# The last image's normalisation: eight rows a group, six groups loaded ahead, buffers of the scan's states, sums on VectorE

## Chip, cores and metric

The kernel runs on one core of a Trainium2 chip. TensorE (PE) multiplies matrices, VectorE (DVE), ScalarE (ACT) and GpSimd (POOL) work elementwise, and SyncE (SP) issues nearly all DMAs here; 16 DMA engines move the data between DRAM and the on-chip memory (SBUF). The metric is the device time of one execution in microseconds (us), lower is better. All data is 32-bit float.

## What is computed

The input `x` has 8 images of 128 channels with 128 x 128 points. Layer 0 (a dilated convolution, an attention over channels in the Fourier domain and a gate) gives a new `x`, which the kernel keeps in DRAM as `x1`, one tensor for each image. Layer 1 is a 3 x 3 convolution, a small state-space scan over 8 tokens of 16 channels at each point, and a group normalisation with SiLU and a residual. The change is at the end of layer 1:

```python
def _L1_conv_ref(x, ...):
    y = conv(x, conv_w) + conv_b
    seq = y.reshape(B * H * W, TOKEN_NUM, GCN)      # 8 tokens of 16 channels
    out = _mamba(seq, ...)                          # the scan
    xr = out.reshape(B, C, H, W)
    g = xr.reshape(B, GROUPS, C // GROUPS, H, W)    # 4 groups
    mu = g.mean((2, 3, 4), keepdims=True)
    var = g.var((2, 3, 4), keepdims=True)
    g = (g - mu) / jnp.sqrt(var + EPS)
    xp = g.reshape(B, C, H, W) * gn_w[None, :, None, None] + gn_b[None, :, None, None]
    xp = jax.nn.silu(xp)
    return x + xp
```

Mean and variance go over a whole image, so no row of an image can be normalised before its last row is out of the scan.

## The kernel before

Channels lie on the 128 partitions. Layer 1 works through 256 blocks of RB = 4 rows (512 elements a partition), 32 blocks an image, in a software pipeline: for each block number i, `step(i, s)` is called for s = 2 to 11 and then `seam(i)`. One call works on several blocks at once; block i is in its scan while i + 3 is in its convolution and i - 1 in its projection out. The loop stands in a manual schedule of all five engines: each engine's instructions keep the order in which the program calls them, and so do SP's DMAs. The loop over i runs from -4 to nb + 1 = 257 (nb = 256). The last block is 255; it leaves the scan in step 256.

The names that matter:

- `project_out` (L881 and on) brings a finished block into `xr` (ScalarE copy, L891). `keep` takes its statistics (VectorE, L898) and stores it to the DRAM tensor `gn` of its image (L899); it is called in the seam of the next block.
- `norm_of(b)` (L902 to L925) is called in step s = 2, two blocks after the last of an image. It makes a scale `sc` and an offset `bi` of the statistics, in small instructions on VectorE, TensorE and ScalarE, and appends the image's 32 blocks to the list `tails`.
- `last_load` takes one block off `tails`: it loads `v` from `gn` (L931) and `res` from `x1` (L932). `last_act` makes SiLU(v * sc + bi) in place on ScalarE (L937). `last_sum` adds it to `res` on GpSimd (L941) and stores `res` to the output (L942). `v` and `res` come from the pool `wk2`, with two buffers of 4 rows each.

During the scan one tail block is done for each scan block: `last_load` at s = 8, `last_act` in the seam, `last_sum` at s = 9 of the next block. So the 32 blocks of image 6 go along with blocks 225 to 256. Image 7, the last, has no scan to go along with: one of its blocks starts in step 257, and the loop `while tails or fin` (L1095), which stands outside the manual schedule and is ordered by the framework's scheduler, does the others. In the built program it comes out in rounds of two blocks: a store, a load of `v`, a store, a load of `v`, then two loads of `res`.

The scan's states `h` and the weighted states `hc` have pools of their own, `hp` and `hcp` (L682, L683), each with seven buffers of 128 partitions x 1024 elements (4 KB a partition). Nothing uses them after the last block's scan.

In both built programs each DMA that SP issues carries one of eight completion semaphores in turn, and where that isn't implied by another wait it waits for the DMA that had the same one before.

Of the kernel before, what the change touches and what calls it, by code (L numbers as in the profile page):

```python
# [9 lines left out]
F32 = mybir.dt.float32  # L10
AF = mybir.ActivationFunctionType
# [5 lines left out]
P = 128  # L17
C = 128
H = 128
W = 128  # L20
# [121 lines left out]
def layer0(ctx, tc, x, w0, c0, x1):  # L142
# [67 lines left out]
    def first_load(p):  # L210
        for b, xt in enumerate(first_rows()):
            nc.vector.memset(xt[:, 0:3, :], 0.0)
            nc.sync.dma_start(xt[:, 3:RX, :], x[2 * p + b, :, 0:RX - 3, :])
# [366 lines left out]
    gram = p_g.tile([P, P], F32, name="gram")  # L580
    E = mybir.EngineType
    with tc.manual_schedule(engines={E.PE, E.Activation, E.DVE, E.Pool, E.SP}):
        first_load(0)
# [6 lines left out]
def layer1(ctx, tc, x1, w1, c1, out):  # L590
# [12 lines left out]
    nc = tc.nc  # L603
# [9 lines left out]
    def cf(name):  # L613
        at, n = C1[name]
        return ct[:, at:at + n]

    def wf(name):
        at, n = W1[name]
        return wt[:, at:at + n]
# [19 lines left out]
    with tc.tile_pool(name="l1_prep", bufs=2) as prep:  # L639
# [18 lines left out]
        for hf in range(NH):  # L658
            for l in range(L):
                k = hf * L + l  # L660
# [14 lines left out]
    RB = 4  # L675
# [6 lines left out]
    hp = ctx.enter_context(tc.tile_pool(name="l1_h", bufs=7))  # L682
    hcp = ctx.enter_context(tc.tile_pool(name="l1_hc", bufs=7))  # L683
# [6 lines left out]
    nb = len(blocks)  # L690
    st8 = [{} for _ in blocks]
    xins, stats, gns, tails = {}, {}, {}, []
# [6 lines left out]
    def misc():  # L699
        return p_m.tile([P, RB, W], F32, name="pm")  # L700
# [67 lines left out]
    def lay_du(i, hf):  # L768


        d = st8[i]
        du = wk2.tile([P, LP, N], F32, name="du")
        for q in range(NG):
            for k, v, g in ((0, d["dt", hf], q), (8, d["u", hf], (q + GP) % NG)):
                nc.sync.dma_start(du[q * DI + k:q * DI + k + 8], v[g * DI:(g + 1) * DI, :])
        d["du", hf] = du
# [125 lines left out]
    def norm_of(b):  # L902

        mv = wk2.tile([P, 2], F32, name="mv")
        gmv = wk2.tile([P, 2], F32, name="gmv")
        dv = wk2.tile([P, 1], F32, name="dv")
        sc = wk2.tile([P, 1], F32, name="sc")
        bi = wk2.tile([P, 1], F32, name="bi")
        nc.vector.bn_aggr(mv, stats[b])
        ps = misc().rearrange("p a b -> p (a b)")  # L910
        nc.tensor.matmul(ps[:, 0:2], cf("group"), mv, start=True, stop=True)
        nc.vector.tensor_copy(gmv, ps[:, 0:2])
        nc.vector.tensor_sub(dv, mv[:, 0:1], gmv[:, 0:1])
        nc.vector.tensor_mul(dv, dv, dv)
        ps = misc().rearrange("p a b -> p (a b)")
        nc.tensor.matmul(ps[:, 0:1], cf("group"), dv, start=True, stop=True)
        nc.vector.tensor_scalar(sc, ps[:, 0:1], gmv[:, 1:2], GN_EPS, ALU.add, ALU.add)
        nc.scalar.activation(sc, sc, AF.Sqrt)
        nc.vector.reciprocal(sc, sc)
        nc.vector.tensor_mul(sc, sc, wf("gn_w"))  # L920
        nc.vector.tensor_mul(bi, gmv[:, 0:1], sc)
        nc.vector.tensor_sub(bi, wf("gn_b"), bi)
        tails.extend((b, r, sc, bi) for r in range(0, H, RB))

    fin = {}  # L925

    def last_load():
        b, r, sc, bi = tails.pop(0)
        v = wk2.tile([P, RB, W], F32, name="v")
        res = wk2.tile([P, RB, W], F32, name="res")  # L930
        nc.sync.dma_start(v, gns[b][:, r:r + RB, :])  # L931
        nc.sync.dma_start(res, x1[b][:, r:r + RB, :])  # L932
        fin["loaded"] = b, r, sc, bi, v, res

    def last_act():
        b, r, sc, bi, v, res = fin["active"] = fin.pop("loaded")
        nc.scalar.activation(v, v, AF.Silu, bias=bi, scale=sc)  # L937

    def last_sum():
        b, r, sc, bi, v, res = fin.pop("active")  # L940
        nc.gpsimd.tensor_add(res, res, v)  # L941
        nc.sync.dma_start(out[b, :, r:r + RB, :], res)  # L942
# [86 lines left out]
    def seam(i):  # L1029


        now, nxt = live(i), live(i + 1)

        def taps(k0, k1):
            if live(i + 3):
                conv(i + 3, k0, k1)

        spreads([(i, 13)], [(i + 1, 1)])
        exps(i, 13)
        if now:  # L1040
            ends_sum(i, 1)
            decay(i, 12)
            add(i, 12)
            weigh(i, 11, 5)
            weigh(i, 12, 7)
        if nxt:
            lay_states(i + 1, 1, 0)
        taps(5, 6)
        if "loaded" in fin:
            last_act()  # L1050
        if live(i + 2):
            project_x(i + 2)
        if now:
            decay(i, 13)
            add(i, 13)
            weigh(i, 13, 7)
        inject(i + 1, 1)
        if live(i + 2):
            project_z(i + 2)
        spreads([(i, 14)], [(i + 1, 2)])  # L1060
        exps(i, 14)
        if now:
            ends_inputs(i, 1)
        if live(i - 1):
            keep(i - 1)
        inject(i + 1, 2)
        taps(6, 8)
        spreads([(i, 15)], [(i + 1, 3)])
        exps(i, 15)
        if now:  # L1070
            collect(i, 4)
            last_decay(i, 14)
            weigh(i, 12, 6)
        inject(i + 1, 3)
        taps(8, 9)
        if now:
            last_decay(i, 15)
        spreads([(i + 1, 2)], [(i + 1, 4)])
        exps(i + 1, 2)
        inject(i + 1, 4)  # L1080
        if now:
            collect(i, 5)
            weigh(i, 13, 6)
        if live(i + 3):
            turn(i + 3)
        if nxt:
            lay_du(i + 1, 1)

    E = mybir.EngineType
    with tc.manual_schedule(engines={E.PE, E.Activation, E.DVE, E.Pool, E.SP}):  # L1090
        for i in range(-4, nb + 2):
            for s in range(2, 12):
                step(i, s)
            seam(i)
    while tails or fin:  # L1095
        if "active" in fin:
            last_sum()
        elif "loaded" in fin:
            last_act()
        else:  # L1100
            last_load()


def network(tc, x, w0, w1, c0, c1, out):
    B = x.shape[0]
    with tc.tile_pool(name="dram", bufs=1, space=DRAM) as dram:
        x1 = [dram.tile([C, H, W], F32, name=f"x1_{b}") for b in range(B)]
        layer0(tc, x, w0, c0, x1)
        layer1(tc, x1, w1, c1, out)
# [73 lines left out]
```

## Time and profile before

| | us |
|---|---|
| median of three runs | 14719.64 (14719.61 to 14726.95) |
| the profiled execution | 14712.15 |
| its span, first to last instruction | 14710.4 |
| last block's `xr` copied out (ScalarE, L891) | 14577.85 to 14578.44 |
| `sc` and `bi` ready (VectorE, L922) | 14584.02 |
| first load of image 7's `v` issued (SP, L931) | 14578.84 |
| end of the span | 14710.4 |

The profile is one execution. All times in it are counted from the span's start. A stretch table gives for each stretch of time how long each engine was busy; the chain of waits follows the work that ended last backwards, from each instruction to what released it. Lines such as L941 are lines of the kernel before.

Around the turn from scan to tail, SP's own list of issues reads (start, length of the issue, engine, line, operation, destination and source, count):

```profile
14574.26 0.34 SPq L942 DMA_DIRECT2D out<-res  x1
14578.47 0.32 SPq L899 DMA_DIRECT2D gn<-xr  x1
14578.84 0.42 SPq L931 DMA_DIRECT2D v<-gn  x1
14579.35 0.40 SPq L932 DMA_DIRECT2D res<-x  x1
14581.93 0.34 SPq L942 DMA_DIRECT2D out<-res  x1
14582.36 0.38 SPq L931 DMA_DIRECT2D v<-gn  x1
```

The first store is of the last block but one of image 6, the second line is block 255 going to `gn`, then come the loads of the first block of image 7, the store of image 6's last block, and the next load.

### The profile page before, as it was taken

How to read it: one execution, taken by the hardware profiler on the slowest of the kernel's cores; microseconds unless marked ns; L12 is line 12 of the kernel's file. 1: busy time of each engine (PE TensorE's matmuls, PEld its weight loads, DVE VectorE, ACT ScalarE, POOL GpSimd, SP SyncE). 2: the span in 40 equal slices, each digit the busy share in tenths (PEclk: the TensorE clock that was granted, in tenths of full speed). 3: DMA queues.
4: the chain of work that ended last, by engine and by line, in shares of the span. 5: the costliest groups of instructions: out<-in, count | busy, mean ns of one | idle time of the engine just before them, and what ended most of it. 6: DMA issues, size and time to landing. Idle time of an engine off the chain costs nothing. (4 is left out here: it accounts for less than half of the span.)

```text
span 14710.4 us, 200914 instructions
## 1 busy us (share of the span) xinstructions
PE 14255.2 (97%) x70696; PEld 5593.5 (38%) x70696; DVE 12679.2 (86%) x12417; ACT 8295.0 (56%) x9234; POOL 12984.8 (88%) x7076
## 2 busy tenths in 40 slices
PE   9999999999999999999999999999999999999996
PEld 6676653333333333333333333333333333333331
DVE  3343359999999999999999999999999999999995
ACT  3354355555656565555556565656556565656553
POOL 6666669999999999999999999999999999999996
PEclk9999999999999999999999999999999999999996
DMA  4444456666666666666666666666666666666665
GB/s 136 140 136 125 129 123 121 120 122 121 134 135 137 139 134 138 135 139 133 139 135 138 135 138 137 135 140 134 138 136 138 135 138 136 135 137 136 138 135 140
DMA packets 1091886, 1976.02 MB, mean 134 GB/s; under 512 B 125760, under 2 KB 256832, under 8 KB 1082688
## 3 DMA queue, kind: packets, MB, share of 16 engines
q1 hardware_dynamic: 1090304, 1960.82, 61.7%
q8 instruction: 563, 9.22, 0.2%
q14 instruction: 443, 3.63, 0.1%
q10 hardware_dynamic: 576, 2.35, 0.0%
HBM read 419.16 MB, written 201.33 MB: 42 GB/s over the span
## 5 line engine op out<-in xcount | busy, mean ns | idle before, releaser
L846 POOL TENSOR_TENSOR hc<-h,cc 128x1024 f32<-128x1024 f32 x3584 | 8375.5, 2368 | 257.5 <-DVE h L840 223.9
L806 ACT ACTIVATE da<-da 128x1024 f32<-128x1024 f32 x3584 | 3618.7, 1010 | 4024.4 <-PE ups L801 2347.3
L816 DVE TENSOR_TENSOR h<-ups,bb 128x1024 f32<-128x1024 f32 x3584 | 4362.1, 1217 | 239.6 <-PE ups L801 164.6
L801 PE MATMUL ups<-du,m_u 16*128 16x512 f32 x14336 | 4118.2, 642 | 3.1 <-DMA du<-u 1.2
L801 PE MATMUL da<-du,m_a 16*128 16x512 f32 x14336 | 4064.6, 643 | 3.7 <-DVE h L840 2.6
L840 DVE TENSOR_TENSOR h<-da,h 128x1024 f32<-128x1024 f32 x2304 | 2820.5, 1224 | 79.1
L832 DVE TENSOR_TENSOR da<-da,h 128x1024 f32<-128x1024 f32 x2304 | 2819.4, 1224 | 4.6 <-ACT da L806 1.1
L134 PE MATMUL pm<-xin,l_wt 128*128 128x508 f32 (+1 forms) x4608 | 2411.0, 623 | 176.8 <-ACT xr L891 170.1
L838 POOL TENSOR_TENSOR h<-ah,h 128x1024 f32<-128x1024 f32 x768 | 1818.6, 2368 | 442.3 <-DVE ah L830 402.2
L801 PEld LDWEIGHTS da<-du,m_a 16*128 16x128 f32 x14336 | 1078.1, 184 | 2467.3 <-issue 1018.1
L867 PE MATMUL yps<-hc,l_ct 128*32 128x512 f32 x14336 | 1929.1, 610 | 1.0 <-POOL hc L846 1.0
L134 PEld LDWEIGHTS pm<-xin,l_wt 128*128 128x128 f32 x4608 | 751.0, 189 | 1618.3 <-issue 1393.5
L801 PEld LDWEIGHTS ups<-du,m_u 16*128 16x128 f32 x14336 | 1130.0, 183 | 372.6 <-DVE h L816 319.4
L806 ACT ACT_TABLE_LOAD x774 | 993.0, 1283 | 30.2 <-PE ups L801 1.3
L830 DVE TENSOR_TENSOR ah<-da,h 128x1024 f32<-128x1024 f32 x768 | 931.6, 1213 | 0.0
L851 DVE TENSOR_TENSOR hc<-da,hc 128x1024 f32<-128x1024 f32 x512 | 623.8, 1218 | 281.2 <-ACT da L806 280.3
L759 POOL TENSOR_TENSOR u<-dt,xc 128x512 f32<-128x512 f32 x512 | 653.4, 1276 | 186.5 <-ACT dt L754 186.5
L867 PEld LDWEIGHTS yps<-hc,l_ct 128*32 128x32 f32 x14336 | 283.7, 108 | 1375.9 <-issue 816.1
L754 ACT ACT_TABLE_LOAD x511 | 655.6, 1283 | 33.1 <-PE pm L752 5.1
L823 POOL TENSOR_TENSOR cb<-bb,cc 128x512 f32<-128x512 f32 x512 | 656.6, 1282 | 11.7 <-DMA cc<-bc 11.7
L886 PEld LDWEIGHTS pm<-m_o,ym 128*128 128x128 f32 x4096 | 517.6, 191 | 317.2 <-issue 316.5
L752 PE MATMUL pm<-xc,m_dt 128*128 128x512 f32 x1024 | 584.7, 653 | 1.5 <-issue 0.8
(180 smaller groups left out, 14528.9 us busy)
## 6 DMA issues: line engine op xcount, KB each, us to landing
bb<-bc SPq DMA_DIRECT2D x2048, 256.0 KB
cc<-bc SPq DMA_DIRECT2D x2048, 256.0 KB
du<-dt SPq DMA_DIRECT2D x2048, 64.0 KB
du<-u SPq DMA_DIRECT2D x2048, 64.0 KB
xin<-x SPq DMA_DIRECT2D x152, 768.0 KB
xin<-x SPq DMA_DIRECT2D x112, 640.0 KB
gn<-xr SPq DMA_DIRECT2D x256, 256.0 KB
v<-gn SPq DMA_DIRECT2D x256, 256.0 KB
```

Of the source, the lines that this page charges most:

```text
L134: nc.tensor.matmul(out[:, a:b, wa:wb], wt[:, t, :], src[:, r + dy + a - base:r + dy + b - base, wa + dx:wb + dx], start=(n == 0), stop=(n ...
L754: nc.scalar.activation(d["dt", hf], ps, AF.Softplus, bias=wf("dt_b"))
L801: nc.tensor.matmul(o, w, v, start=True, stop=True)
L806: nc.scalar.activation(da, da, AF.Exp)
L816: nc.vector.tensor_mul(h, d["ups", s], state_row(i, "bb", s // GP))
L823: nc.gpsimd.tensor_mul(d["cb", hf], d["bb", hf][:, lp, :], d["cc", hf][:, lp, :])
L830: nc.vector.tensor_mul(d["ah"], da, before)
L832: nc.vector.tensor_mul(da, da, before)
L838: nc.gpsimd.tensor_add(h, d["ah"], h)
L840: nc.vector.tensor_add(h, d["da", s], h)
L846: nc.gpsimd.tensor_mul(hc, d["h", s], state_row(i, "cc", t))
L867: nc.tensor.matmul(d["yps"][g * DI:(g + 1) * DI], gather[:, t % LP, :], d["hc", GP * t + g // GP][:, g % GP], start=False, stop=(t in (3, ...
```

## The change

The loop over i ends at nb = 256, so step 257 is gone. What is left of image 6 (its last block, loaded and activated in step and seam 256) is summed and stored first, in a short loop on `fin`. Image 7 is then done in 16 groups of TR = 8 rows (1024 elements a partition, 512 KB each): `tail_load` loads a group into one buffer of `hp` (under the name `h`) and one of `hcp` (`hc`); `tail` makes the SiLU on ScalarE, the sum on VectorE in place of GpSimd, and the store. Six groups are loaded before `norm_of` is called; after each group's store the group six further on is loaded. All of it stands in the manual schedule, so SP issues in the written order.

```diff
--- before.py
+++ after.py
@@ -1086,19 +1086,47 @@
         if nxt:
             lay_du(i + 1, 1)
 
+
+    TR = 2 * RB
+    ends_of = [(nb // (H // RB) - 1, r) for r in range(0, H, TR)]
+    held = {}
+
+    def tail_load(k):
+        if k < len(ends_of):
+            b, r = ends_of[k]
+            v = hp.tile([P, TR, W], F32, name="h")
+            res = hcp.tile([P, TR, W], F32, name="hc")
+            nc.sync.dma_start(v, gns[b][:, r:r + TR, :])
+            nc.sync.dma_start(res, x1[b][:, r:r + TR, :])
+            held[k] = v, res
+
+    def tail(k, sc, bi):
+        (b, r), (v, res) = ends_of[k], held.pop(k)
+        nc.scalar.activation(v, v, AF.Silu, bias=bi, scale=sc)
+        nc.vector.tensor_add(res, res, v)
+        nc.sync.dma_start(out[b, :, r:r + TR, :], res)
+
+    AHEAD = 6
     E = mybir.EngineType
     with tc.manual_schedule(engines={E.PE, E.Activation, E.DVE, E.Pool, E.SP}):
-        for i in range(-4, nb + 2):
+        for i in range(-4, nb + 1):
             for s in range(2, 12):
                 step(i, s)
             seam(i)
-    while tails or fin:
-        if "active" in fin:
-            last_sum()
-        elif "loaded" in fin:
-            last_act()
-        else:
-            last_load()
+        while fin:
+            if "active" in fin:
+                last_sum()
+            else:
+                last_act()
+        assert not tails
+        for k in range(AHEAD):
+            tail_load(k)
+        b = ends_of[0][0]
+        norm_of(b)
+        _, _, sc, bi = tails[0]
+        for k in range(len(ends_of)):
+            tail(k, sc, bi)
+            tail_load(k + AHEAD)
 
 
 def network(tc, x, w0, w1, c0, c1, out):
```

## Prediction

> **What bounds the kernel now.** For most of the span TensorE, VectorE and GpSimd are all nearly full, and the change touches none of that work. It touches the last image's normalisation, so I looked only at the end of the span. I read the stretch table first, then the chain of waits, then the waits and the instruction groups of the end, then the stretch table again for what the DMA engines can do.
>
> Stretch table (one row per stretch: its length, busy time and count of each engine, granted clock, mean busy share of the 16 DMA engines, GB/s moved):
>
> ```profile
> core 0: us, PE busy (x) PEld busy (x) DVE busy (x) ACT busy (x) POOL busy (x), PEclk, DMA share, GB/s
> 14600.00:14650.00 50.00, 0.00 (x0) 0.00 (x0) 0.00 (x0) 10.66 (x14) 15.54 (x13) 0.50 0.64 203
> ```
>
> In the last 125 us TensorE and VectorE do nothing, ScalarE and GpSimd are busy a fifth and a third of the time, and the DMA engines 64%. No engine is full: the end is a chain of latencies. The chain of waits shows one round of it, of two four-row blocks (start, length, what):
>
> ```profile
> 14604.81 2.73 DMA out<-res
> ...
> 14607.62 3.24 DMA res<-x
> ...
> 14610.89 1.88 POOL res L941 x2
> ...
> 14612.79 0.38 SPq L942
> ...
> 14613.26 0.45 SPq L931
> ...
> 14613.75 4.22 DMA res<-x
> ```
>
> A store must land (2.73 us) before its `res` buffer can be loaded again (3.24 us); then the two adds run, then the two stores go out. With two buffers of each kind the loads cannot run ahead of the stores. A round takes 7.9 us (the add after a DMA wait starts at 14610.28, the next such at 14618.13) for 6 x 256 KB. The waits and groups of the end, from 14590 us on, say the same:
>
> ```profile
> ACT v L937 <- DMA v<-gn: 93.2, 30, 4.9
> POOL res L941 <- DMA res<-x: 80.6, 16, 5.7
> L941 POOL TENSOR_TENSOR res<-res,v 128x512 f32<-128x512 f32 x30 | 37.4, 1262 | 80.7 <-DMA res<-x 80.6
> L937 ACT ACTIVATE v<-v,bi,sc 128x512 f32<-128x512 f32 x30 | 24.4, 812 | 93.2 <-DMA v<-gn 93.2
> ```
>
> Both compute engines wait for DMA for most of the 120 us. What the DMA engines give when work is queued deep shows at the very start of the span (first two rows), where six loads of 4.5 and 6 KB a partition run back to back, beside the constants. The third row is one 256 KB store alone at the end, the fourth the densest mixture of loads and stores there:
>
> ```profile
> 4.00:8.00 4.00, 0.00 (x0) 0.00 (x0) 1.89 (x10) 0.30 (x2) 0.00 (x0) 1.00 1.02 417
> 8.00:12.00 4.00, 3.44 (x8) 1.08 (x10) 3.56 (x12) 0.00 (x0) 3.18 (x3) 1.00 1.03 426
> 14612.50:14613.00 0.50, 0.00 (x0) 0.00 (x0) 0.00 (x0) 0.00 (x0) 0.26 (x1) 0.50 1.04 406
> 14652.00:14654.00 2.00, 0.00 (x0) 0.00 (x0) 0.00 (x0) 0.00 (x0) 0.00 (x0) 0.50 1.00 293
> ```
>
> So one direction alone runs at 406 to 426 GB/s, and today's mixture at about 293 when the engines are full.
>
> **What the Trainium skill says.** "DMA: Bandwidth & Descriptors", Bandwidth, Measured: a 1 MB load alone reaches 341 GB/s and a 16 MB one 425, so size and depth hide the fixed cost; the start of this trace agrees with the upper figure (417 to 426). The same page, Anatomy of one DMA: the fixed cost is about 2 us, mostly the receipt of the last byte, and a semaphore wait is done by the issuing sequencer, not by the DMA engines. The trace agrees: a 256 KB store takes 2.73 us to release its buffer, where its bytes alone take 0.65 us at 406 GB/s. "HBM Reference", Specifications: a core that streams alone goes well above its half of the domain, about 425 GB/s; one core runs here, and 417 to 426 agrees.
>
> **The change part by part.**
>
> *Bytes.* They stay: 32 blocks x 3 x 262144 B = 25.17 MB (x 16 groups of twice the size after). The row run per partition grows from 2 to 4 KB.
>
> *Start of the stream.* Before, the first block of the last image is loaded in step 257, and SP issues that load at 14578.84, ahead of the store of the image before's last block (14581.93). After, step 257 is gone, and on SP all loads stand behind that store, which waits for GpSimd's add (14580.64 to 14581.90), which waits for ScalarE's table load and SiLU behind `xr`. None of this moves. So the first load goes out at 14581.93 + 0.34 = 14582.3, 3.5 us later than now: a small loss. Its bytes flow some 0.8 us later (a store issued at 14603.53 shows in the DMA share from about 14604.3): 14583.1. The words "ahead of the norm" hold little: the norm's last instruction (`bi`, L922) ends at 14584.0, so it was never what was waited for.
>
> *Depth.* Twelve loads are asked for at once. In the built order each DMA from SP takes one of eight completion semaphores in turn and waits for the one eight places before, so eight are in flight, 4.2 MB or over 10 us of work at 400 GB/s. SP's issues cost about 0.47 us each with the gap (0.43 for the 576 KB loads at the start): 48 x 0.47 = 23 us, hidden.
>
> *The added waits on SP.* The order becomes store k, load v of k+6, load res of k+6. Store k waits for VectorE's add k, and the loads behind it for it; but add k needs loads that stand 16 DMAs earlier in the queue, landed long before by the rule of eight. The `res` load of k+6 takes the buffer of k-1 and waits for that store to land; the store stands five DMAs ahead of it, so four DMAs (2.1 MB, over 5 us) are still queued while its receipt and the new start take 2 us. The queue never runs dry, at the end neither: when the last load lands, five stores are behind it.
>
> *Compute.* ScalarE: 16 SiLUs of 128x1024. The trace has 812 ns for 512 elements and, for L754 against L738 (512 and 1024 from PSUM), 688 and 1116, a step of 428 ns: 1.24 us each, 20 us. VectorE: 16 adds; "VectorE: DVE Perf Modes", TRN2 errata, prices an fp32 `tensor_tensor` at (N+151)/0.96 ns, 1224 ns for 1024, and the trace has 1224 for L840: 20 us on an engine that is idle there. GpSimd loses 32 x 1.26 us of adds that nobody but this tail waits for. All lies under the stream; the cover is three times as long. If it were gone, the first group's SiLU and add (2.5 us) would show once.
>
> *Rate.* No row shows 512 KB loads and stores of 4 KB runs mixed deep. From below: 293 GB/s, today's densest window (2 KB runs, directions switching every 256 KB). From above: 420, the start. Larger runs and half as many switches speak for more than 293, the stores for less than 420; I take the midpoint, 356.
>
> *Sum.* 25.17 MB / 356 GB/s = 70.7 us, and 2.0 us from the last byte to the end of the span (the last store's 256 KB, issued at 14706.9, would be through by 14708.4; the span ends at 14710.4). 14583.1 + 70.7 + 2.0 = 14655.8, against 14710.4: **-54.6 us**. At 293: 85.9 us, -39.4. At 420: 59.9, -65.4. The profiled execution took 14712.15, 7.5 below the median of the three runs (14719.64); the difference is taken off the median: 14665.
>
> **Rivals.**
>
> A. *The mixture stays slow.* The stretch between the dead times today, e.g. 14604 to 14607, moves only about 260 GB/s at a share of 0.82, with switches between directions as one possible cause. If switching is what costs and depth doesn't help, the rate stays at 255 to 290: 98.7 to 86.8 us, -26.6 to -38.5, that is 14681 to 14693. Against: the share there is below 1, so it isn't full.
>
> B. *A new wait takes the old one's place.* If SP's in-order waits (store for add, `res` load for a store's landing) do drain the queue, each of the 16 groups keeps a hole like today's 3.2 us of 7.9 (dead time between the last load and the next store's bytes): 16 x 3.2 = 51 us given back, 14716, no change. For it: SP is one queue and stores stand before loads. Against: the count of DMAs behind each wait above.
>
> C. *Slower.* One mechanism: stores whose rows lie 64 KB apart in DRAM, queued deep, go slowly. "DMA: Bandwidth & Descriptors", Latency and other measured facts, gives 103 to 207 GB/s for tiles with row pitches of 512 KB to 8 MB. Loads at 420 need 40 us for 16.8 MB; the tail has 14710.4 - 14583.1 - 2.0 = 125.3 us, so the 8.4 MB of stores turn the change into a loss from 85.3 us on, below 98 GB/s; at 80 it would be 105 us, 14739. Against: the loads at the start have this pitch and run at 420, and a lone store ran at 406.
>
> **How the numbers follow.** Forecast 0.81, A 0.12, B 0.05, C 0.02. 0.2% of the median is 29.4 us, about what a measurement of this kernel tells from no change; it is reached at 264 GB/s. The forecast's whole range lies beyond it, and of A three quarters, of B a fifth: faster 0.81 + 0.09 + 0.01 = 0.91, same 0.07, slower 0.02. Range: the forecast's own 14654 to 14680, 4 us more on either side for the spread of runs (14719.6 to 14726.9), and the nearer part of A: 14650 to 14688.
>
> **What would show it.** Right: stretches of 10 us from 14590 on with a DMA share near 1 and 330 to 400 GB/s; ScalarE and VectorE still waiting for loads, but the chain of waits a run of DMA with nothing of GpSimd; first load on SP near 14582.3; at the end five stores in a row. Wrong: stretches below 290 GB/s at a share of 1 (A), a share of 0.6 to 0.8 with SP waiting for stores or adds (B), stores that take far longer to land than loads of the same size (C). A change before 14574 us would mean that the edit reaches further than the tail.

## Result and the profile after

| | before | after |
|---|---|---|
| median of six runs, us | 14720.09 (14717.56 to 14726.95) | 14656.55 (14655.21 to 14664.52) |
| ratio to before | | 0.9957 (95%: 0.9945 to 0.9970) |
| profiled execution / its span, us | 14712.15 / 14710.4 | 14655.59 / 14653.8 |
| block 255's `xr` copied out (end of L891), us | 14578.4 | 14584.8 |
| from there to the end of the span: the tail, us | 132.0 | 69.0 |

The change takes 63.5 us off the median. The two profiled executions are 56.6 us apart only, because the scan of this one ended 6.4 us later. The tail, which is all that the change touches, lost 63.0 us; it is the measure of all experiments below. The end of the scan moves by up to 17 us between the profiled executions of this study, and the tail can be read without that. Taken off the medians, the tails leave 14588.1 us before and 14587.6 after, so nothing suggests that the edit reaches the scan. Each tail is read from one profiled execution, and its own spread was not measured: differences of a microsecond or two between tails are not told apart below.

The stretch table of the changed kernel (columns as before: length, busy times and counts, clock, DMA share, GB/s):

```profile
14595.00:14600.00 5.00, 0.00 (x0) 0.00 (x0) 3.10 (x3) 2.90 (x3) 0.00 (x0) 0.50 1.02 418
14605.00:14610.00 5.00, 0.00 (x0) 0.00 (x0) 1.85 (x2) 1.24 (x1) 0.00 (x0) 0.50 0.97 365
14610.00:14650.00 40.00, 0.00 (x0) 0.00 (x0) 12.25 (x10) 12.40 (x10) 0.00 (x0) 0.50 1.03 419
14646.00:14650.00 4.00, 0.00 (x0) 0.00 (x0) 0.68 (x1) 0.00 (x0) 0.00 (x0) 0.50 1.02 417
```

Where it was 203 GB/s at a share of 0.64, it is now 419 GB/s for 40 us on end, loads and stores mixed, as fast as loads alone at the start of the span. The last row is stores alone: the last load had landed before the last sum began at 14645.45. ScalarE and VectorE work under a third of the time. The one dip is the first round in which SP waits for a store to land. SP's issues of the changed kernel around it:

```profile
14588.29 0.34 SPq L942 DMA_DIRECT2D out<-res  x1
14588.72 0.39 SPq L1099 DMA_DIRECT2D h<-gn  x1
...
14597.98 0.34 SPq L1107 DMA_DIRECT2D out<-hc  x1
...
14603.11 0.32 SPq L1099 DMA_DIRECT2D h<-gn  x1
14609.04 0.32 SPq L1100 DMA_DIRECT2D hc<-x  x1
14609.45 0.44 SPq L1107 DMA_DIRECT2D out<-hc  x1
```

The first load goes out right behind image 6's last store. The `res` load at 14609.04 is the eighth group's. It takes the buffer of the first group, so it stood from 14603.4 on until the first group's store (14597.98) had landed, that is, until its completion was reported, 11 us after its issue. Up to seven DMAs of 512 KB were in front of that store; with its own bytes they make 4.2 MB, by estimate 10 us at 410 GB/s. The chain of waits is now a row of such store landings, 7 us each, with nothing of GpSimd in it:

```profile
14613.52 6.73 DMA out<-hc
...
14620.68 7.06 DMA out<-hc
...
14628.16 7.08 DMA out<-hc
```

It looks like latency, as it did before, but the 419 GB/s beside it, the rate of loads alone, says that these stores wait in a full queue. Each link of this chain carries two groups (a store lands, the `res` load of its buffer goes out, and right behind it the store two groups further on): 3.15 MB in 7.5 us, which is 420 GB/s.

### The profile page after: what moved, and what is told of

It reads as the page before. It is cut to its first block, busy times and chain, and to the rows that moved or that the text cites. A ratio compares the mean times of both kernels' runs of the same rounds, so it can differ in the third digit from the quotient of the medians.

```text
span 14653.8 us, 200772 instructions
## 1 busy us (share of the span) xinstructions
PE 14260.3 (97%) x70696; PEld 5597.0 (38%) x70696; DVE 12701.0 (87%) x12433; ACT 8286.6 (57%) x9218; POOL 12941.2 (88%) x7044
## 5 line engine op out<-in xcount | busy, mean ns | idle before, releaser
L840 DVE TENSOR_TENSOR h<-da,h 128x1024 f32<-128x1024 f32 x2304 | 2821.3, 1225 | 79.1
L832 DVE TENSOR_TENSOR da<-da,h 128x1024 f32<-128x1024 f32 x2304 | 2820.4, 1224 | 4.2 <-ACT da L806 1.1
```

Of the source, the lines that this page charges most:

```text
L832: nc.vector.tensor_mul(da, da, before)
L840: nc.vector.tensor_add(h, d["da", s], h)
```

## Experiments

Two theories could explain the gain. **Depth**: more bytes are in flight, whatever their size. **Size**: runs of 4 KB and DMAs of 512 KB, which switch between loading and storing half as often, are faster by themselves. The first four runs cross the two.

**Four rows, six ahead.**

```diff
-    TR = 2 * RB
+    TR = RB
-            v = hp.tile([P, TR, W], F32, name="h")
-            res = hcp.tile([P, TR, W], F32, name="hc")
+            v = hp.tile([P, 2 * RB, W], F32, name="h")[:, 0:TR, :]
+            res = hcp.tile([P, 2 * RB, W], F32, name="hc")[:, 0:TR, :]
```

> The tail is measured within the profile, from SP's issue of block 255's store to gn (L899) to the end of the span: 131.9 us before, 69.0 us after. Here groups have four rows (2 KB a partition, 256 KB a DMA) as before the change, still six groups ahead, all else as in the change. Theory depth (the gain comes from DMAs queued ahead, 2.1 MB under the rule of eight, whatever their size): the engines stay full at 400 GB/s or nearly, tail 69 to 74 us. Theory size (the rate of the mixture rises with 4 KB runs and fewer switches between loads and stores): the rate falls to today's densest 293 GB/s, 85.9 us of stream and some 8 more, tail 92 to 96 us.

Measured: tail 84.3 us, between the two. The stretch table and SP's waits of this run (engine and line, what it waited for, us in total, times, longest):

```profile
14600.00:14640.00 40.00, 0.00 (x0) 0.00 (x0) 11.70 (x17) 13.31 (x17) 0.00 (x0) 0.50 0.98 332
```

```profile
SPq L1100 <- DMA out<-hc: 20.0, 17, 2.8
```

The rate is 332 GB/s although the DMA share is 0.98, and SP stands half of the 40 us before `res` loads whose buffer still belongs to a store. Neither theory foresaw this. The wait alone is no proof of a loss: in the changed kernel SP stands 23.4 of the same 40 us before such loads, at 410 GB/s:

```profile
SPq L1100 <- DMA out<-hc: 23.4, 9, 4.7
```

The chain of waits of the four-row run tells more. It is again a row of store landings:

```profile
14612.61 4.37 DMA out<-hc
...
14617.41 4.48 DMA out<-hc
```

From 14603.41 to 14632.17 it has six links of 4.8 us on the mean. Each carries two groups of four rows, 1.57 MB, and that makes 328 GB/s, close to the 332 of the stretch table. At 410 GB/s the bytes would pass in 3.8 us: here the landing sets the pace.

**Eight rows, two ahead; four rows, two ahead; eight rows, one ahead.** The edits are `AHEAD = 2` or `AHEAD = 1`, for the second with the four-row edit above.

> Groups of eight rows, but two groups ahead in place of six. Theory depth: a load goes out after the add two groups earlier, with its store in front of it; 0.9 us of issue, 0.8 to the first byte, 3.8 us for 1.5 MB, 1.0 to land, 1.2 for the add make 7.6 us for two groups, 3.8 us a group, just at the DMA limit: tail 69 to 78 us. Theory size: 69 to 71 us.

> Groups of four rows and two ahead, the nearest to the old loop in size and depth, but in written order, with seven buffers (so no load waits for a store to land) and the sums on VectorE. Theory depth: 0.9 + 0.8 + 1.9 + 1.0 + 0.7 = 5.3 us for two groups, 2.65 us a group, 32 groups 85 us and some 8 more: tail 90 to 97 us, where the old loop takes 131.9. Theory size: the same 92 to 96 us, so it is told apart by the first run, not by this one. If the old loop's order and two buffers cost nothing of their own, the tail stays at 125 to 132 us.

> Groups of eight rows and one ahead: a load goes out only after the add of the group before it, behind its store. Theory depth: each group has the whole 7.6 us to itself, 16 x 7.6 = 122 us and some 8 more: tail 125 to 132 us, as long as before the change. Theory size: the stores still overlap and the rate is that of large runs, tail 69 to 85 us.

| | rows | ahead | tail, us | GB/s, 14600 to 14640 |
|---|---|---|---|---|
| before the change | 4 | 2 buffers | 132.0 | 202 |
| the change | 8 | 6 | 69.0 | 410 |
| first run | 4 | 6 | 84.3 | 332 |
| second run | 8 | 2 | 88.6 | 318 |
| third run | 4 | 2 | 98.7 | 291 |
| fourth run | 8 | 1 | 132.7 | 205 |

With one group ahead the groups of eight rows are as slow as the old loop (expected by depth: 125 to 132; by size: 69 to 85). Size, written order and sums on VectorE therefore bring nothing together as long as the depth is missing. One round of this run moves 1.57 MB in 7.7 us, a round of the old loop the same bytes in 7.9. With two ahead both sizes come out slower than worked out: 88.6 in place of 69 to 78 at eight rows, 98.7 in place of 90 to 97 at four. At eight rows the groups come in pairs, and SP waits for their sums. This is seen in the timeline of the second run:

```profile
14619.84 0.34 SPq L1107 DMA_DIRECT2D out<-hc  x1
...
14623.54 0.34 SPq L1107 DMA_DIRECT2D out<-hc  x1
...
14630.09 0.34 SPq L1107 DMA_DIRECT2D out<-hc  x1
```

Two stores 3.7 us apart, then a gap of 6.5: 10.2 us for two groups, where the sum had 7.6. The chain of waits shows what the sum missed (a load of `v`, then SiLU, then sum):

```profile
14624.00 7.23 DMA h<-gn
...
14631.32 1.25 ACT h L1105
...
14632.59 1.24 DVE hc L1106
```

The sum had left out the SiLU, and the load takes 7.2 us where 0.8 + 3.8 + 1.0 = 5.6 were reckoned. At one ahead the same 7.6 us came near the measured 7.7 by luck: there load and issue take 5.2 us where 6.5 were reckoned, which makes up for the SiLU.

**Runs of 2 KB in DMAs of 512 KB.** Why is four rows slower at six ahead? This run keeps all sizes of the change, but takes a group's eight rows from two places (the load of `res` and the store are changed likewise):

```diff
-    ends_of = [(nb // (H // RB) - 1, r) for r in range(0, H, TR)]
+    ends_of = [(nb // (H // RB) - 1, r) for r in range(0, H // 2, RB)]
+
+    def halves(t, r):
+        return t.rearrange("c (a h) w -> c a h w", a=2)[:, :, r:r + RB, :]
-            nc.sync.dma_start(v, gns[b][:, r:r + TR, :])
+            nc.sync.dma_start(v.rearrange("c (a h) w -> c a h w", a=2), halves(gns[b], r))
...
```

> The first run (four rows, six ahead) gave 326 GB/s at a DMA share of 0.97 and a tail of 84.3 us, against 404 GB/s and 69.0 us for the change. This run tells what of it is the length of the run and what the size of the DMA: groups of eight rows, 512 KB a DMA, six ahead as in the change, but each group is four rows of the upper half of the image and four of the lower, so that a partition's data comes in two runs of 2 KB. Theory run length (a 2 KB run costs the engines more time per byte): 320 to 340 GB/s, tail 82 to 86 us. Theory DMA size (each DMA costs something at its end, or 256 KB pieces put too little in flight): 400 GB/s, tail 69 to 71 us.

Measured: 407 GB/s, tail 70.8 us. (The 326 GB/s above are the first run's from 14600 to 14650; the table has 332 up to 14640.) The length of the run is cleared. What is left is something that comes with the 256 KB DMA.

**Four rows, five ahead.** `AHEAD = 5` with the four-row edit.

> Run five cleared the 2 KB runs (407 GB/s in DMAs of 512 KB), so the 326 GB/s of four rows and six ahead comes with the 256 KB DMAs. Two causes are left. Wait for a store: with seven buffers and six ahead, a res load takes the buffer of a store that stands five DMAs before it and waits for it to land; of 256 KB DMAs only four lie behind that, 1 MB, too little to bridge the landing. Cost per DMA: each DMA costs the engines something at its end. Five ahead in place of six puts the store eight DMAs before the load, so that the rule of eight alone limits what is in flight. Theory store wait: the rate rises to 380 to 410 GB/s and the tail falls from 84.3 to 69 to 75 us, though fewer groups are loaded ahead. Theory cost per DMA: nothing gained, 82 to 87 us.

Measured: tail 71.0 us. The stretch table and the longest of SP's waits:

```profile
14600.00:14640.00 40.00, 0.00 (x0) 0.00 (x0) 15.23 (x22) 17.06 (x21) 0.00 (x0) 0.50 1.05 402
```

```profile
SPq L1107 <- DMA h<-gn: 5.6, 19, 0.4
SPq L1100 <- DMA out<-hc: 5.2, 19, 0.3
```

One group fewer ahead, 13.3 us faster. The waits for stores fall from 20.0 us to 5.2. So the small DMA itself costs little or nothing (402 GB/s against 410): the change's group of eight rows matters mainly in that it makes six ahead out of seven buffers harmless. With 256 KB DMAs and six ahead, the load that waits for the store two turns back has only 1 MB queued behind that store, too little; with five ahead the store is three turns back. Why the DMA share stayed at 0.98 in the slower of the two runs isn't shown.

**Sums on GpSimd.**

```diff
-        nc.vector.tensor_add(res, res, v)
+        nc.gpsimd.tensor_add(res, res, v)
```

> The change with the sums back on GpSimd (128x1024, 2.37 us each by the rows of that size). Theory DMA-bound: the sums lie under 3.8 us of DMA a group; only the last one is seen, +1.2 us at most: tail 69 to 71 us. Rival, that a slower sum delays the stores and with them the loads behind them on SP: 16 x 1.2 = 18 us, tail 80 to 88 us.

Measured: tail 69.9 us, 409 GB/s. GpSimd is busy 26.9 of the 40 us from 14600 on, and it doesn't show. The tail is 0.9 us longer, which one profile each can't tell from no change. It is not the last group's sum, as was expected: that sum ends at 14648.03, and the queued stores still keep the DMA engines at 418 GB/s from 14648 to 14650. With six ahead, the move to VectorE is worth nothing that can be told apart here.

**The kernel before with seven buffers.**

```diff
         b, r, sc, bi = tails.pop(0)
-        v = wk2.tile([P, RB, W], F32, name="v")
-        res = wk2.tile([P, RB, W], F32, name="res")
+        if b < B - 1:
+            v = wk2.tile([P, RB, W], F32, name="v")
+            res = wk2.tile([P, RB, W], F32, name="res")
+        else:
+            v = hp.tile([P, GP * RB, W], F32, name="h")[:, 0:RB, :]
+            res = hcp.tile([P, GP * RB, W], F32, name="hc")[:, 0:RB, :]
```

> The kernel before with one edit: the last image's v and res take the seven buffers of h and hc (four rows of each); the order is left to the framework's scheduler, step 257, four-row blocks and GpSimd's sums stay. Theory depth from buffers alone: the scheduler itself brings the loads some six blocks forward, and the tail is that of the four-row run, 84.3 us, less up to 3.5 us for the first loads that do not wait for image 6's last store: 80 to 86 us. Rival, that the written order or VectorE's faster sum carries a good part: 95 to 125 us.

Measured: tail 94.7 us, so the buffers alone bring 37.3 of the 63.0 us. The expectation was missed because the depth isn't what I took it for: in the built order the scheduler begins with four loads of `v` ahead of the first store, and from the fifth store on it keeps two blocks ahead, though seven buffers are there. Two ahead in written order gave 98.7 (third run); the difference of 4.0 is near the 3.5 us by which the first loads go out earlier here, since they don't stand behind image 6's last store. The two runs differ in the engine of the sums as well (1.26 us on GpSimd, 0.70 on VectorE), so this comparison isn't clean. The rest of the gain came only with the written order and its greater depth: 71.0 us at four rows and five ahead, with the sums on VectorE. What the sums alone are worth at four rows was not run.

**Loads in step 256.** The stream fills the tail, so it should start earlier:

```diff
             for s in range(2, 12):
+                if i == nb and s == 9:
+                    for k in range(AHEAD):
+                        tail_load(k)
                 step(i, s)
...
-        for k in range(AHEAD):
-            tail_load(k)
```

> The change with the twelve first loads moved up on SP: after the last load of image 6 (step 256, s = 8), ahead of the store of image 6's last block but one, of block 255's store and of image 6's last store. They then wait only for the scan to let go of its buffers, which GpSimd and TensorE do one by one in the last 8 us of the scan. Theory DMA-bound: the stream of 61 us starts up to 15 us earlier; measured from the end of the xr copy of block 255 to the end of the span the tail falls from 69.0 to 54 to 58 us, the time by 11 to 15 us to 14642 to 14646. Rival, that the norm (ready 5.6 us after the xr copy) or the loads' waits on SP hold back the first stores, or that the loads disturb the end of the scan: a gain of 0 to 6 us.

Measured: 14647.45 us (14644.74 to 14648.98), ratio to before 0.9949 (0.9936 to 0.9963), 9.1 us below the change's median, and the ranges of the two don't overlap; tail 60.3 us. The gain lies between the two expectations. It is less than worked out, for two reasons that the profile shows. SP's issues:

```profile
14565.44 0.38 SPq L1099 DMA_DIRECT2D h<-gn  x1
14576.91 0.32 SPq L1100 DMA_DIRECT2D hc<-x  x1
14577.32 0.38 SPq L1099 DMA_DIRECT2D h<-gn  x1
...
14595.51 0.34 SPq L1107 DMA_DIRECT2D out<-hc  x1
```

```profile
14595.00:14600.00 5.00, 0.00 (x0) 0.00 (x0) 5.00 (x6) 4.89 (x5) 0.00 (x0) 0.50 0.86 261
```

The first buffer of `hc` comes free only at 14576.9, 10 us before the `xr` copy ends (14586.9). And all six groups are in before the norm is done; the first store goes out at 14595.51, and the stretch from 14595 to 14600 moves 261 GB/s. The norm, which cost nothing before, is now late: its last instruction ends at 14592.45, and the first SiLU starts at 14592.99, when ScalarE has also loaded its table.

**A seventh group ahead.** The edit against the run before:

```diff
                 if i == nb and s == 9:
-                    for k in range(AHEAD):
+                    for k in range(AHEAD + 1):
                         tail_load(k)
...
             tail(k, sc, bi)
-            tail_load(k + AHEAD)
+            if k > 0:
+                tail_load(k + AHEAD)
```

> Run eight has its loads in step 256 and gave a tail of 60.3 us; between 14595 and 14600 us its DMA engines moved 261 GB/s only, since the six groups were loaded before the norm let the first store go. Here a seventh group is loaded ahead too (the seventh buffer), and the loads after the stores go on in the old order, one group later. Theory DMA-bound with a hole: 1 MB more to move in the hole of about 2 us, tail 57.5 to 59.5 us, time 14644 to 14648. Rival, that the hole is moved on and not filled (the seventh group's res load waits on SP for its buffer): 60 to 61 us, no change.

Measured: 14648.34 us (14645.0 to 14650.5), just outside the 14644 to 14648 expected, and a tail of 59.3 us, within 57.5 to 59.5. The stretch table:

```profile
14595.00:14600.00 5.00, 0.00 (x0) 0.00 (x0) 5.00 (x5) 4.16 (x4) 0.00 (x0) 0.50 1.03 413
14600.00:14605.00 5.00, 0.00 (x0) 0.00 (x0) 0.51 (x2) 1.24 (x1) 0.00 (x0) 0.50 0.98 311
```

The hole is filled where it was and comes back 5 us later, where SP waits for the first store to land. In the tail 1 us may be left of it, in the time nothing that can be told from the run before. The loads in step 256, with six groups or seven, give the best times found, and they beat both kernels.

## The prediction, point by point

*What bounded the tail* was right: a chain of latencies with DMA engines that were not full. The fourth run shows it from the other side, since one group ahead brings the old time back with everything else of the change in place.

*The start of the stream* was right: predicted 3.9 us from the end of the `xr` copy to the first load, measured 3.9. That the norm was never waited for was right as well; it became late only when the loads were moved into step 256.

*Compute* was right: 1239 ns for the SiLU (worked out 1.24 us), 1225 ns for the sum (1224), and both hidden. That GpSimd's sums covered nothing holds at this depth: moving them back changed nothing that can be told apart (0.9 us). When only two groups are ahead, SiLU and sum are no longer hidden (second run).

*Depth and the added waits on SP* were right in their outcome at this size. Eight DMAs in flight was the limit only at the start. Later the wait for a store's landing came first (23.4 us of 40), and then only that store and the four DMAs behind it were in flight. "Never runs dry" was too strong: the queue ran low once, at 14605 to 14610. The count of bytes behind the store names the right quantity, but its 2 us for receipt and new start are too few. At 400 GB/s they ask for only 0.8 MB, so 256 KB DMAs with 1 MB behind the store would have passed, and there the same order loses 15 us.

*The rate* is the term that was off. The sum took 356 GB/s, the midpoint of 293 and 420, and 70.7 us of stream. The predicted tail was 14655.8 - 14578.4 = 77.4 us, the measured one 69.0; the 8.4 us between them are this term: from 14589.5 (first load and 0.8) to 14651.8 (2.0 before the end) the 25.17 MB took 62.3 us, 404 GB/s on the mean. The lower bound was misread. I took 293 GB/s at a DMA share of 1.00 for full engines, but the share counts the time that packets are under way. The runs of four rows with six and with five ahead have the same DMAs and nearly the same share (0.98 and 1.05), at 332 and 402 GB/s. The upper end, 420, would have been the better guess, and the sign named for being right, 330 to 400 GB/s, was passed. So the gain was 63 us where 54.6 were predicted, and the time 14656.55 where 14665 was, in the range of 14650 to 14688.

*Rivals.* A (the mixture stays slow) is refuted by 419 GB/s over 40 us of loads and stores, and C (stores slow) by 417 GB/s of stores alone (14646 to 14650). B (SP's order drains the queue) is refuted for this kernel, and real for 256 KB DMAs with six ahead. Two figures of the rivals were off. The hole of 3.2 us in B isn't in the trace, where the DMA engines move next to nothing only from about 14610.3 to 14612.3, 2 us. And 0.2% of the median is reached at 262 GB/s, not 264. Neither changes a verdict.

*Figures taken over.* The 341 GB/s and the fixed 2 us of the Trainium skill ("DMA: Bandwidth & Descriptors", Measured and Anatomy of one DMA) are stated there for DMAs that GpSimd issues; here SP issues them. Its 103 to 207 GB/s in rival C (same page, Latency and other measured facts) are of copies between DRAM tensors, with 214 as the full rate, so they say little about stores from SBUF. The measurements decide: 2.73 us for a 256 KB store, 417 GB/s for stores with rows 64 KB apart.

## What to carry to other kernels

When a tail is made of load, compute, store with all DMA engines partly idle, count the bytes that are queued behind each wait on the issuing queue and compare them with what flows in a landing time; buffers, order and DMA size are three ways to the same number of bytes in flight. More buffers alone brought 37 of 63 us here, since the scheduler used two of seven, and with 256 KB DMAs six groups ahead in place of five cost 13 us, because a load then waits for too recent a store. Behind such a store 1 MB of queued DMAs was too little here, 1.8 and 2.1 MB were enough; where the limit lies between them was not measured. Once such a stream is full, its start is what is left to move: here 9 us.

## What the hardware showed that I hadn't expected

Loads and stores mixed on one queue ran at 419 GB/s, as fast as loads alone (417 to 426); switching between directions cost nothing visible, and 2 KB runs (407) and 256 KB DMAs (402) cost little or nothing, once enough was queued. A DMA share near 1 is not a full engine: shares of 0.97 to 1.05 went with anything from 293 to 426 GB/s. A 512 KB store in the full queue took 7 to 11 us to release its buffer, where a 256 KB store took 2.7 us in the old loop.
